# Small first groups and a denser opening weave in a sparse graph-attention layer

## The chip, the core and the metric

The kernel runs on one core of a Trainium2 chip. The metric is the device time of one execution in microseconds (us); lower is better. The engines are PE (TensorE, matrix products), DVE (VectorE), ACT (ScalarE), POOL (GpSimd) and SP (SyncE, which here only issues transfers). Each takes its own instructions strictly in the order in which the program lists them, and waits for the others through semaphores.

## The reference, cut to what matters

One layer of graph attention over 4096 nodes with 512 features, and then a norm. A target row attends to the source rows that `adj` connects it to: about 16 of 4096, itself included.

```python
hs = layer_norm(h_source); ht = layer_norm(h_target)        # h_source is x
q, k, v = ht @ Wq, hs @ Wk, hs @ Wv                          # 8 heads of 64
logits = einsum('thd,shd->hts', q / 8, k), -1e30 where adj == 0
ctx = einsum('hts,shd->thd', softmax(logits), v)
ht = layer_norm(ht + ctx @ Wo)
ht = ht + gelu(ht @ W1) @ W2                                 # 512 -> 2048 -> 512
out = _layernorm(x + ht)
```

Everything is float32.

## The kernel before

**Stages.** In the first 280 us PE computes the rows of keys and values of all 4096 source nodes and ACT writes them to a table in memory, `kvd` (4 KB for each node: key, then value). Beside this the kernel reads the dense `adj` and makes a list of neighbours of each target row; the rows of the first half of the targets (part A) are then sorted by their number of neighbours and cut into 16 tiles of 128 rows. A tile has a cap, the largest number of neighbours in it. The tiles are taken in the order of caps 11, 13, 14, 15, 15, 16, 17, 17, 18, 19, 19, 20, 22, 23, 24, 39 and then the 16 tiles of part B. Tiles are numbered from 0 in this order.

**Attention of a tile** (`attention`, with `front`, `issue`, `values` and `finish`). For each neighbour slot POOL issues one gather of 128 rows of `kvd` (L987, 512 KB) into a ring of slots, 17 of them for part A. Three slots make a segment. For a segment DVE multiplies keys with the query `tq` (L1258) and sums over each head (L1263); ACT takes the exponent (L1267, or L1276 for a tile's first segment); DVE multiplies two slots' values with it (L1219), and ACT the third slot's, head by head (`by_scalar`, L1239 and L1242). PE adds the values up by transposing them into one PSUM tile, `cps` (L1230, four for each slot), and only after that may the slot be gathered into again. The query comes from `front`: a gather (L987, `tq`), two PE steps (transposes L1030, product with `wq` L1040) and an add on DVE (L1045).

**The end of a tile** is `finish`: sums and reciprocal on DVE (L1115, L1118, L1121, L1122), a copy on ACT (L1125), four PE transposes (L1131), a copy on ACT (L1133), the scaling on DVE (L1136), the product with `wo` on PE (L1142, L1146), a copy on ACT (L1151) and the statistics of the norm on DVE (L697, L698). When the last tile of a group is there, the norm follows: L680 on DVE, a power on POOL (L687), L692 on DVE, L1164 on ACT, transposes on PE (L1173) and a copy into `h2T` on ACT (L1177).

**Feed-forward of a group** (`feed`). `_order` makes the groups: the first tile alone, then pairs. A group's `h2T` goes through W1 (L1367, `pf`), gelu on ACT (L1370) and W2 (L1376, into `po`), and `end` adds `x`, norms and writes the rows out. A pair has eight blocks with 256 columns, a group of one has four with 128 columns.

**Order.** No engine chooses. `_weave` runs four generators (attention, feed-forward, the lists of the rest of part B, the last weight loads) in the order of a written clock: each `yield` tells how much the piece before it costs, and the generator with the least sum is next. A pair's attention costs 60 (`UNIT`), and so does its feed-forward; a feed-forward whose `h2T` isn't made yet sleeps. `yield`s without a number inside `finish` and `front` put their next step behind further attention work. After that a scheduler fixes each engine's list; `tc.issue_after` (here `behind`) puts an instruction behind another on its engine. `other_lists` starts at clock 94 (`WAIT`), and each of its steps costs 2.2 times its own figure. `weights` loads the third quarter of W1 and W2 at clock 26 and the fourth at 36, each as two transfers of 1 MB from ACT's queue.

Of the kernel before, what the change touches and what calls it, by code (L numbers as in the profile page):

```python
# [12 lines left out]
ALU = mybir.AluOpType  # L13
# [371 lines left out]
def _order():  # L385


    n, m = len(CAPS_A), len(CAPS_B)
    a = [(k * P, c) for k, c in enumerate(CAPS_A)]
    b = [((n + k) * P, c) for k, c in enumerate(CAPS_B)]  # L390
    groups = [[a.pop()]]
    while len(a) > 1:
        groups.append([a.pop(), a.pop()])
    groups.append(a + [b.pop()])
    while len(b) > 1:
        groups.append([b.pop(0), b.pop()])
    return groups + [b]
# [46 lines left out]
def adj_resnorm_kernel(  # L444
# [88 lines left out]
    with tc.tile_pool(name="keep", bufs=1) as keep:  # L533
# [17 lines left out]
        with ExitStack() as late:  # L551
# [429 lines left out]


            recs, tqs, h2Ts, done, ready, latest, newest = {}, {}, {}, set(), [], [], []
            issues, logits = [], []

            def gather(dst, table, idx):
                issues[:] = [nc.gpsimd.indirect_dma_start(  # L987
# [121 lines left out]
            def finish(i, p, cps, group, hs, mv):  # L1109


                rec, tq, cap = recs[i], tqs.pop(i), TILES[i][1]
                slow = 0 if i < QUICK else 1

                nc.vector.scalar_tensor_tensor(p[:, :cap, :], rec[:, E0:E0 + cap].unsqueeze(2)  # L1115
                                               .to_broadcast([P, cap, H]), 0.0, p[:, :cap, :],
                                               op0=ALU.is_gt, op1=ALU.mult)
                nc.vector.tensor_reduce(sums[:, i, :], p[:, :cap, :].rearrange("p j h -> p h j"),  # L1118
                                        AX.X, ALU.add)
                ri = sp.tile([P, H], F32, name="ri")  # L1120
                nc.vector.tensor_scalar_max(ri, sums[:, i, :], SUM_LO)  # L1121
                nc.vector.reciprocal(ri, ri)  # L1122
                rx = sp.tile([P, KC, P], F32, name="rb", bufs=1)
                rxf = rx.rearrange("p c t -> p (c t)")
                nc.scalar.copy(rxf.rearrange("p (h d) -> p h d", h=H),  # L1125
                               ri.unsqueeze(2).to_broadcast([P, H, HD]))
                for _ in range(1 + 1 * slow):
                    yield
                prx = ps.tile([P, KC, P], F32, name="t", bufs=2)
                for c in range(KC):  # L1130
                    nc.tensor.transpose(prx[:, c, :], rxf[:, c * P:(c + 1) * P], ident)  # L1131
                ct = sp.tile([P, KC, P], F32, name="rb", bufs=1)
                nc.scalar.copy(ct, prx)  # L1133
                for _ in range(1 + 1 * slow):
                    yield
                nc.vector.tensor_mul(ct, cps, ct)  # L1136
                for _ in range(1 + 3 * slow):
                    yield
                pa = ps.tile([P, D], F32, name="t", bufs=2)

                for c in range(KC):
                    nc.tensor.matmul(pa[:, c * P:(c + 1) * P], tq[:, D + c * P:D + (c + 1) * P],  # L1142
                                     ident, is_transpose=True, start=c == 0, stop=False,
                                     skip_group_check=True)
                for c in range(KC):
                    nc.tensor.matmul(pa, ct[:, c, :], wo[:, c, :], start=False,  # L1146
                                     stop=c == KC - 1, skip_group_check=True)
                turned.add(i)
                yield
                h = sp.tile([P, D], F32, name="h")  # L1150
                nc.scalar.copy(h, pa)  # L1151
                yield
                stats(sp, h, mv[:, len(hs), :], "n2")
                hs.append(h)
                if len(hs) < len(group):
                    return
                nh = len(hs)
                ve = shifted(sp, mv[:, :nh, :], nh, "n2")
                yield
                rs = power(sp, mv[:, :nh, :], nh, "n2", ve)  # L1160
                yield
                nm = negmean(sp, mv[:, :nh, :], rs, nh, "n2")
                for j, h in enumerate(hs):
                    nc.scalar.activation(h, h, AF.Identity, bias=nm[:, j:j + 1], scale=rs[:, j:j + 1])  # L1164
                for _ in range(1 + 1 * slow):
                    yield
                w = len(hs) * P
                h2T = sp.tile([P, KC, 2 * P], F32, name="h2T")
                for k2 in range(KC // 2):
                    pt = ps.tile([P, 2, 2 * P], F32, name="t", bufs=2)  # L1170
                    for k in range(2):
                        for j, h in enumerate(hs):
                            nc.tensor.transpose(pt[:, k, j * P:(j + 1) * P],  # L1173
                                                h[:, (k2 * 2 + k) * P:(k2 * 2 + k + 1) * P], ident)
                    for k in range(2):
                        kc = k2 * 2 + k
                        nc.scalar.activation(h2T[:, kc, :w], pt[:, k, :w], AF.Identity,  # L1177
                                             bias=b2c[:, kc:kc + 1], scale=s2c[:, kc:kc + 1])
                h2Ts[GROUPS.index(group)] = h2T
# [22 lines left out]
            def attention():  # L1202
# [44 lines left out]
                for group in GROUPS:  # L1247
                    hs = []
                    mv = sp.tile([P, 2, 2], F32, name="mv2")
                    cost = 0.5 * UNIT * len(group) / 2 / sum(TILES[i][1] for i in group)  # L1250
                    for i in group:
                        cps = ps.tile([P, KC, P], F32, name="cps", bufs=2)
                        while k < len(SG) and SG[k][0] == i:
                            _, j0, n = SG[k]
                            while i not in tqs:
                                step(fronts, i)
                            kv, tq = kvs.pop(k), tqs[i]
                            nc.vector.tensor_tensor(kv[:, :n, :D], kv[:, :n, :D],  # L1258
                                                    tq[:, :D].unsqueeze(1).to_broadcast([P, n, D]),
                                                    ALU.mult)  # L1260
                            lg = sp.tile([P, S, H], F32, name="lg")
                            latest[:] = [lg[:, 0, 0:1]]
                            logits[:] = [nc.vector.tensor_reduce(  # L1263
                                lg[:, :n, :], kv[:, :n, :D].rearrange("p j (h d) -> p j h d", h=H),
                                AX.X, ALU.add).ins]
                            if j0 > 0:
                                nc.scalar.activation(p[:, j0:j0 + n, :], lg[:, :n, :], AF.Exp)  # L1267
                            advance()
                            yield cost * n
                            if pend:  # L1270
                                values(*pend.pop())
                                request(k)
                            advance()
                            if j0 == 0:
                                p = sp.tile([P, MAXE, H], F32, name="p", bufs=1)
                                nc.scalar.activation(p[:, :n, :], lg[:, :n, :], AF.Exp)  # L1276
                            if n == S:
# [142 lines left out]
                for g in gens:  # L1420
                    yield from g

            WAIT = 94.0
            AHEAD = 4
            ADDS = 11
            HEAVY = 30
            DENSE = 21
            QUICK = 7
            UNIT = 60.0

            ed = all_edges()
            steps = 2 * NQ + 1
# [57 lines left out]
            def weights():  # L1490


                for q, pool in enumerate(pools):
                    yield 26.0 if q == 0 else 10.0
                    with tc.issue_after(newest[-1]):
                        load_quarter(pool, q + 2, nc.scalar)

            def other_lists():
                for _ in range(2):
                    adjs.append(quarter(*divmod(len(adjs), NQ)))  # L1500
                yield 6.0
                for cost in ed:
                    yield 2.2 * cost
                keep_rest()
                yield from sort(1)

# [37 lines left out]
```

## Time and profile before

| | us |
|---|---|
| median of 3 runs (1791.04 to 1794.76) | 1792.74 |
| the profiled execution | 1786.53 |
| its span in the trace | 1784.8 |
| PE, DVE, ACT, POOL busy in the span | 1663.4, 1422.9, 1236.9, 1005.6 |
| POOL's gathers of `kvd`, 603 of them | 785.6 |

The profiled execution ran 1.7 us beside its span, and 6.2 us (0.35%) under the median of the runs shown. Busy times are unions of recorded spans on one engine. Matmul records overlap, since the next one starts before the last has left the array; a stretch in which PE is busy all the time is one in which it never waited, but the record's length isn't what a matmul costs. That cost is the distance between two starts in a row of equal matmuls. Each float32 product is recorded as two matmuls; a transpose is one.

### The profile page before, as it was taken

Reading aid. Unit: us, or ns where it says so; the run is one execution under the profiler, and the core shown is the slowest. Engines: PE = TensorE matmul, PEld = TensorE weight load, DVE = VectorE, ACT = ScalarE, POOL = GpSimd, SP = SyncE. Lnnn points to the kernel's source line nnn. Section 1 sums busy time; section 2 is a strip of 40 time slices with the busy share of each in tenths; the row PEclk is TensorE's granted clock in tenths of the full one; section 3 lists DMA queues with packets and bytes.
Section 4 is the critical chain, followed back from the end, with each engine's and each line's share of the span. In section 5 each row is a group of like instructions: output and inputs, shape, how many; then the busy total and the mean of one; then the engine's idle time right before and its main releaser. Section 6 shows DMA issues by size and latency. Waiting matters only on the chain. (4 is left out here: it accounts for less than half of the span.)

```text
span 1784.8 us, 22466 instructions
## 1 busy us (share of the span) xinstructions
PE 1663.4 (93%) x6850; PEld 1074.3 (60%) x6850; DVE 1422.9 (80%) x2447; ACT 1236.9 (69%) x3131; POOL 1005.6 (56%) x822
## 2 busy tenths in 40 slices
PE   7989994889999999898888999999999999999997
PEld 3434443656666766665555766666666666656665
DVE  6888787879688989897878888989888888987500
ACT  5776663667777878676667877787878777876511
POOL 1000156765556666677777688866686766665101
PEclk9999997899999999999999999999999999999999
DMA  9999988978778798767777798987777867665000
GB/s 350 362 391 367 360 269 304 336 242 282 268 256 299 272 316 277 248 205 252 243 273 272 244 316 286 304 278 237 246 257 247 298 218 255 233 230 189 20 5 26
DMA packets 141610, 461.00 MB, mean 258 GB/s; under 512 B 18036, under 2 KB 23048, under 8 KB 141480
## 3 DMA queue, kind: packets, MB, share of 16 engines
q0 software_dynamic: 96272, 342.33, 56.6%
q1 hardware_dynamic: 37392, 94.06, 14.8%
q10 hardware_dynamic: 7816, 23.08, 3.3%
q8 instruction: 57, 0.93, 0.2%
q14 instruction: 73, 0.60, 0.1%
HBM read 430.61 MB, written 28.79 MB: 257 GB/s over the span
## 5 line engine op out<-in xcount | busy, mean ns | idle before, releaser
L987 POOL DMA_INDIRECT kv<-kvd,rec x603 | 785.6, 1303 | 342.2 <-issue 117.4
L1367 PE MATMUL pf<-h2T,w 128*128 128x256 f32 (+1 forms) x2176 | 473.7, 371 | 3.4 <-ACT h2T L1177 3.4
L1376 PE MATMUL po<-w,gt 128*128 128x512 f32 x1024 | 465.4, 596 | 2.7 <-ACT gt L1370 2.7
L1367 PEld LDWEIGHTS pf<-h2T,w 128*128 128x128 f32 x2176 | 391.1, 193 | 72.5 <-issue 22.2
L1258 DVE TENSOR_TENSOR kv<-kv,tq 128x1536 f32<-128x1536 f32 (+2 forms) x211 | 351.9, 1677 | 66.7 <-DMA kv<-kvd,rec 54.0
L1242 ACT ACTIVATE kv<-kv,pa 128x64 f32<-128x64 f32 x1520 | 390.7, 336 | 4.4
L1263 DVE TENSOR_REDUCE lg<-kv 128x24 f32<-128x1536 f32 (+2 forms) x211 | 350.4, 1667 | 0.3
L1376 PEld LDWEIGHTS po<-w,gt 128*128 128x128 f32 x1024 | 188.2, 191 | 196.8 <-issue 192.8
L1230 PE MATMUL cps<-ident,kv 128*128 128x128 f32 x1828 | 245.6, 280 | 51.9 <-DVE kv L1219 34.1
L1230 PEld LDWEIGHTS cps<-ident,kv 128*128 128x128 f32 x1828 | 216.7, 144 | 127.6 <-DVE kv L1219 40.6
L1219 DVE TENSOR_TENSOR kv<-kv,p 128x1024 f32<-128x1024 f32 (+1 forms) x211 | 251.2, 1192 | 25.2 <-ACT p L1267 23.7
L687 POOL TENSOR_TENSOR n_rs<-n_ve,mhalf 128x2 f32<-128x2 f32 (+2 forms) x51 | 53.5, 1049 | 338.7 <-DVE n_ve L680 155.1
L735 ACT ACTIVATE kv<-kv 128x1024 uint8<-128x1024 int32 x128 | 134.5, 1053 | 60.1 <-DMA kv<-in_adj_dram 24.3
L1370 ACT ACT_TABLE_LOAD x109 | 139.8, 1283 | 1.8
L1370 ACT ACTIVATE gt<-pf 128x512 f32<-128x512 f32 x128 | 76.4, 597 | 88.2 <-PE pf L1367 84.9
L1146 PE MATMUL t<-wo,rb 128*128 128x512 f32 x256 | 120.0, 610 | 7.9 <-DVE rb L1136 7.9
L949 PE MATMUL pq<-wk,h2T 128*128 128x512 f32 x256 | 118.8, 607 | 4.2 <-DMA wk<-in_L_gnn_Wk_dram 2.9
L949 PE MATMUL pq<-wv,h2T 128*128 128x512 f32 x256 | 117.3, 601 | 4.2 <-DVE rbc L662 2.9
L1040 PE MATMUL t<-wq,tq 128*128 128x512 f32 x256 | 115.4, 593 | 2.4 <-ACT tq L1033 2.4
L744 DVE MAX8 cand<-kv 128x8 uint16<-128x171 uint16 (+1 forms) x384 | 108.0, 324 | 1.2
L1267 ACT ACTIVATE p<-lg 128x24 f32<-128x24 f32 (+2 forms) x179 | 39.0, 218 | 100.3 <-DVE lg L1263 99.4
L1267 ACT ACT_TABLE_LOAD x71 | 91.1, 1283 | 1.2
(164 smaller groups left out, 1534.6 us busy)
## 6 DMA issues: line engine op xcount, KB each, us to landing
kv<-in_adj_dram SPq DMA_DIRECT2D x128, 512.0 KB, 6.8
kvd<-tq ACTq DMA_DIRECT2D x23, 512.0 KB, 7.0
kv<-kvd,rec POOLq DMA_INDIRECT x603, 5.9
kv<-in_L_gnn_h_target_dram SPq DMA_DIRECT2D x32, 256.0 KB, 7.2
kv<-in_x_dram SPq DMA_DIRECT2D x15, 512.0 KB, 8.3
kvd<-kv ACTq DMA_DIRECT2D x9, 512.0 KB, 7.0
w<-in_L_gnn_W_dram SPq DMA_DIRECT2D x4, 1024.0 KB, 7.2
w<-in_L_gnn_W_dram ACTq DMA_DIRECT2D x4, 1024.0 KB, 15.4
```

Source lines behind the costliest of these rows:

```text
L735: nc.scalar.activation(sg, a, AF.Sign, accum_out=dpart[:, i, h:h + 1])
L949: nc.tensor.matmul(pkv, hT[:, kc, j * P:(j + 1) * P], w[:, kc, :], start=kc == 0, stop=kc == KC - 1)
L987: issues[:] = [nc.gpsimd.indirect_dma_start(out=dst, out_offset=None, in_=table[:, :], in_offset=bass.IndirectOffsetOnAxis(ap=idx, axis=0) ...
L1219: nc.vector.tensor_tensor(v4, v4, p[:, j0:j0 + m, :].unsqueeze(3) .to_broadcast([P, m, H, HD]), ALU.mult)
L1230: nc.tensor.matmul(cps[:, c, :], kv[:, j, D + c * P:D + (c + 1) * P], ident, is_transpose=True, start=j0 + j == 0 and c == 0, stop=j0 + n ...
L1242: newest[:] = [nc.scalar.mul(v, v, pa[:, hd:hd + 1]).ins]
L1258: nc.vector.tensor_tensor(kv[:, :n, :D], kv[:, :n, :D], tq[:, :D].unsqueeze(1).to_broadcast([P, n, D]), ALU.mult)
L1263: logits[:] = [nc.vector.tensor_reduce(lg[:, :n, :], kv[:, :n, :D].rearrange("p j (h d) -> p j h d", h=H), AX.X, ALU.add).ins]
L1267: nc.scalar.activation(p[:, j0:j0 + n, :], lg[:, :n, :], AF.Exp)
L1367: nc.tensor.matmul(pf[:, k, :], w1[(f0 + k) // KC][:, kc, (f0 + k) % KC * P:((f0 + k) % KC + 1) * P], h2T[:, kc, :w], start=kc == 0, stop= ...
L1370: nc.scalar.activation(gt, pf, AF.Gelu_apprx_tanh)
L1376: nc.tensor.matmul(po[j], gt[:, k, j * P:(j + 1) * P], w2[(f0 + k) // KC][:, (f0 + k) % KC, :], start=False, stop=f0 + k == FC - 1, skip_g ...
```

## The change

Five edits.

1. `_order` makes three groups of one tile (0, 1 and 2) and then pairs. Groups are now 0 / 1 / 2 / 3,4 / 5,6 and so on: the pair 1,2 is split, and from 3,4 on every group holds the same tiles as before. There is one group more, 18 for 17.
2. In `finish`, tile 0 has no `yield` between its first steps, and tiles 0 to 2 have two fewer later.
3. Tile 0's reciprocal and scaling are remembered in `closing`; the next product of keys is put behind the reciprocal, the next sum over heads behind both, and then the list is emptied.
4. For groups that start with tiles 1 to 8, the clock's cost of attention is multiplied by 0.7 (tiles 1 to 4) or 0.85 (tiles 5 to 8).
5. `WAIT` goes from 94 to 70, the factor of the lists from 2.2 to 1.9, and the fourth quarter of the weights follows the third after 6 and not 10.

```diff
-    groups = [[a.pop()]]
+    groups = [[a.pop()] for _ in range(3)]
     while len(a) > 1:
         groups.append([a.pop(), a.pop()])
...
+                first = i == 0
...
-                nc.vector.reciprocal(ri, ri)
+                recip = nc.vector.reciprocal(ri, ri)
...
-                for _ in range(1 + 1 * slow):
+                for _ in range(0 if first else 1 + slow):
                     yield
...
-                nc.vector.tensor_mul(ct, cps, ct)
-                for _ in range(1 + 3 * slow):
+                scaled = nc.vector.tensor_mul(ct, cps, ct)
+                if first:
+                    closing[:] = [recip.ins, scaled.ins]
+                for _ in range(0 if first else 1 + 3 * slow):
                     yield
...
                 turned.add(i)
-                yield
+                if i > 2:
+                    yield
...
                 ve = shifted(sp, mv[:, :nh, :], nh, "n2")
-                yield
+                if i > 2:
+                    yield
...
                     cost = 0.5 * UNIT * len(group) / 2 / sum(TILES[i][1] for i in group)
+                    if 0 < group[0] < 9:
+                        cost *= PACE[group[0] > 4]
...
-                            nc.vector.tensor_tensor(kv[:, :n, :D], kv[:, :n, :D],
-                                                    tq[:, :D].unsqueeze(1).to_broadcast([P, n, D]),
-                                                    ALU.mult)
+                            with behind(closing[:1]):
+                                nc.vector.tensor_tensor(kv[:, :n, :D], kv[:, :n, :D],
+                                                        tq[:, :D].unsqueeze(1)
+                                                        .to_broadcast([P, n, D]), ALU.mult)
...
-                            logits[:] = [nc.vector.tensor_reduce(
+                            with behind(closing):
+                                logits[:] = [nc.vector.tensor_reduce(
...
+                            closing.clear()
...
-            WAIT = 94.0
+            WAIT = 70.0
+            PACE = (0.7, 0.85)
...
-                    yield 26.0 if q == 0 else 10.0
+                    yield 26.0 if q == 0 else 6.0
...
-                    yield 2.2 * cost
+                    yield 1.9 * cost
```

More of the change, by code (lines that the diff above doesn't have):

```diff
@@ L983, in adj_resnorm_kernel @@
             recs, tqs, h2Ts, done, ready, latest, newest = {}, {}, {}, set(), [], [], []
-            issues, logits = [], []
+            issues, logits, closing = [], [], []
             def gather(dst, table, idx):
@@ L1133, in finish @@
                 nc.scalar.copy(ct, prx)
-                for _ in range(1 + 1 * slow):
+                for _ in range(0 if first else 1 + slow):
                     yield
-                nc.vector.tensor_mul(ct, cps, ct)
-                for _ in range(1 + 3 * slow):
+                scaled = nc.vector.tensor_mul(ct, cps, ct)
+                if first:
+                    closing[:] = [recip.ins, scaled.ins]
+                for _ in range(0 if first else 1 + 3 * slow):
                     yield
@@ L1164, in finish @@
                     nc.scalar.activation(h, h, AF.Identity, bias=nm[:, j:j + 1], scale=rs[:, j:j + 1])
-                for _ in range(1 + 1 * slow):
+                for _ in range(0 if first else 1 + slow):
                     yield
@@ L1257, in attention @@
                             kv, tq = kvs.pop(k), tqs[i]
-                            nc.vector.tensor_tensor(kv[:, :n, :D], kv[:, :n, :D],
-                                                    tq[:, :D].unsqueeze(1).to_broadcast([P, n, D]),
-                                                    ALU.mult)
+                            with behind(closing[:1]):
+                                nc.vector.tensor_tensor(kv[:, :n, :D], kv[:, :n, :D],
+                                                        tq[:, :D].unsqueeze(1)
+                                                        .to_broadcast([P, n, D]), ALU.mult)
                             lg = sp.tile([P, S, H], F32, name="lg")
                             latest[:] = [lg[:, 0, 0:1]]
-                            logits[:] = [nc.vector.tensor_reduce(
-                                lg[:, :n, :], kv[:, :n, :D].rearrange("p j (h d) -> p j h d", h=H),
-                                AX.X, ALU.add).ins]
+                            with behind(closing):
+                                logits[:] = [nc.vector.tensor_reduce(
+                                    lg[:, :n, :],
+                                    kv[:, :n, :D].rearrange("p j (h d) -> p j h d", h=H),
+                                    AX.X, ALU.add).ins]
+                            closing.clear()
                             if j0 > 0:
```

## The prediction

> **What bounds the kernel now.** I read the page's slices first, then a table by stretches, then PE's timeline.
>
> ```profile
> PE   7989994889999999898888999999999999999997
> PEclk9999997899999999999999999999999999999999
> ```
>
> PE is nearly full to the end. The table has, for each stretch, its length and then busy us of PE, weight loads, DVE, ACT and POOL, the granted clock and the DMA share.
>
> ```profile
> 280.00:340.00 60.00, 30.71 (x145) 22.30 (x145) 45.88 (x46) 22.93 (x86) 42.95 (x36) 0.74 0.98 369
> 340.00:380.00 40.00, 40.00 (x225) 28.32 (x224) 28.45 (x29) 24.96 (x69) 23.51 (x20) 1.00 0.62 198
> 380.00:405.00 25.00, 18.32 (x94) 12.93 (x93) 23.43 (x42) 19.52 (x62) 21.14 (x15) 0.85 0.93 336
> 405.00:500.00 95.00, 92.17 (x403) 63.08 (x401) 76.48 (x142) 68.68 (x171) 50.45 (x45) 0.97 0.75 260
> 500.00:590.00 90.00, 90.00 (x409) 62.67 (x408) 77.04 (x134) 69.42 (x181) 57.14 (x47) 1.00 0.82 288
> 740.00:1080.00 340.00, 302.37 (x1347) 208.94 (x1346) 286.84 (x306) 238.24 (x668) 259.37 (x201) 0.96 0.77 260
> 1080.00:1640.00 560.00, 551.17 (x2316) 364.62 (x2315) 488.59 (x560) 427.91 (x1112) 393.60 (x309) 1.00 0.77 256
> 1640.00:1773.00 133.00, 132.68 (x555) 87.91 (x553) 39.33 (x94) 48.02 (x112) 10.23 (x12) 1.00 0.06 20
> ```
>
> PE never waits in 340 to 380, 500 to 590 and after 1640; it waits in 280 to 340, in 380 to 405 and in 740 to 1080, and its clock is then cut too. So the span is PE's work plus PE's lost time, and the change is worth the lost time that it removes. What the work costs is read from PE's timeline, by distances between starts:
>
> ```profile
> 358.88 3.60 PE L1376 MATMUL po<-w,gt 128*128 128x512 f32 x8
> 362.31 1.47 PE L1230 MATMUL cps<-ident,kv 128*128 128x128 f32 x12
> 363.62 3.74 PE L1367 MATMUL pf<-h2T,w 128*128 128x128 f32 x32
> 367.20 3.60 PE L1040 MATMUL t<-wq,tq 128*128 128x512 f32 x8
> ...
> 419.63 3.62 PE L1367 MATMUL pf<-h2T,w 128*128 128x256 f32 x16
> 423.08 1.47 PE L1230 MATMUL cps<-ident,kv 128*128 128x128 f32 x12
> ```
>
> (362.31-358.88)/8 is 0.429 us at 512 columns; likewise 0.109 for a transpose, 0.112 for a product of 128 columns and 0.216 for 256. Multiplying by the counts gives the work ahead of each group's first L1367; start minus work is the time lost by then:
>
> | group | starts | work ahead | lost |
> |---|---|---|---|
> | 0 | 338.0 | 268.6 | 69.4 |
> | 1,2 | 405.3 | 325.8 | 79.5 |
> | 3,4 | 498.7 | 413.1 | 85.6 |
> | 5,6 | 586.8 | 500.9 | 85.9 |
> | 7,8 | 679.9 | 591.1 | 88.8 |
> | 9,10 | 780.7 | 680.4 | 100.3 |
> | last | 1744.4 | 1585.7 | 158.7 |
>
> **What the Trainium skill says.** "Perfetto Trace Analysis", section "Identifying the Most-Contended Engine", calls matmul busy time no good measure; agreed: eight L1376 records of 0.592 us each sit in 3.43 us, hence the distances. "TensorE: Matmul & The Clock Gate", Part 1, "What's actually happening", says that PE's clock halves after an idle window of some 3.4 us; the table shows 0.74 and 0.85 in the two stretches with waits and 1.00 in the full ones. "DMA: Bandwidth & Descriptors", "Queues, rings and completion order", says that an engine takes turns between queues; here ACT's four weight transfers landed after 15.4 us (median) beside gathers, SP's four of the same size after 7.2 us.
>
> **The change, part by part.** I had the order in which each engine of the changed kernel gets its instructions; durations are the profile's. Lines are the kernel's before.
>
> *First tile's end.* DVE's timeline before:
>
> ```profile
> 307.52 1.79 DVE L1258 TENSOR_TENSOR kv<-kv,tq 128x1536 f32<-128x1536 f32 x1 [1.36 <-DMA kv<-kvd,rec]
> 309.24 0.19 DVE L1122 RECIPROCAL ri<-ri 128x8 f32<-128x8 f32 x1
> ...
> 321.41 1.76 DVE L1258 TENSOR_TENSOR kv<-kv,tq 128x1536 f32<-128x1536 f32 x1 [2.31 <-DMA kv<-kvd,rec]
> 323.37 0.69 DVE L1258 TENSOR_TENSOR kv<-kv,tq 128x512 f32<-128x512 f32 x1 [0.20 <-DMA kv<-kvd,rec]
> 323.98 0.68 DVE L1136 TENSOR_TENSOR rb<-cps,rb 128x512 f32<-128x512 f32 x1
> ```
>
> The reciprocal now stands ahead of the product that waits for a gather: 3 us earlier. But the scaling L1136 still stands behind **all four** remaining products of tile 1, the last of which had its data at 323.4; only the sums were moved behind it. With one L1219 (1.22) in between it comes at 325.1, 1.1 us later than before. Then come what was done earlier before: two sums (3.4), two small steps and L1219, a sum, L697, L1219, a sum, L1219. This puts tile 1's fourth segment at 336.5 (it was 328). PE has 44 of tile 1's transposes ahead of L1173; POOL has four gathers ahead of the power, whose slots come free late (power at about 337, was 333.6). So L692 is at 337.7, L1164 ends at 338.7, the copies to `h2T` at 340.9: the first block starts at **341, 3 us later**.
>
> *Tile 2's query.* L1030 and L1040 were ahead of the first block and are now behind its start and behind its 64 matmuls (7.2 us): work ahead is 264.3. L1040 ends at 352 and not 335.8, so tile 2's attention starts 16 us later. Behind it on DVE wait tile 2's products. Lost by the first block: 341-264.3 = 76.7, against 69.4.
>
> *Groups of one.* Before, PE at 380 to 405 has nothing, as 1,2 wait for tile 2. Now PE goes on from 352: W2, two blocks, tile 1's end, tile 2's first three segments, tile 3's query; by distances that is until 386, and each of these has its input in time (tile 2's DVE work from 352.7: values of its segments at 362.8 and 365.7). The norm of tile 1 is ready at about 384, `h2T` at 388, so group 1 starts at 388.5 with 310.1 ahead: lost 78.4. Tile 3's query is ready at 381.9 (371.5 before), tile 4's at 416 (399.7). DVE needs 35.4 us for tile 3 (five segments of 4.7, nine from the lists, the ends 3); PE has 43 us for a tile (28 feed-forward, 6.9 for the two 512-column products, 6.5 for 15 slots, 2 other transposes). So PE stays the slower and group 3,4 starts at 413.3+78.4 = 491.7, **7 us earlier** than 498.7.
>
> *The split pair* costs 2 x 128 x 0.112 against 128 x 0.216: +1.0 us on PE. Gelus are as many; ACT's table loads go from 220 to 224 in the whole program, 1.28 us each, beside a full PE: nothing while ACT isn't late.
>
> POOL gets two powers more (L687, 0.66 us each for one column), and its gathers queue behind each: now behind the 45th, 53rd, 58th and 73rd gather, where it was the 62nd and 69th. The one after 58 waits for tile 2's norm, some 410 by the above; tile 4's second segment, which is behind it, isn't wanted before 420: nothing, +6 at most if that norm is late.
>
> *Denser weave.* From 5,6 on PE's order is nearly the same, except that feed-forward starts up to 10 us of work further behind its `h2T` (5,6: 9.9, was 5.6; 13,14: 19.0, was 10.7). That leaves blocks to fill a wait such as the one at 677 (2.74 us for `h2T`, then half clock, 4.5 lost in 660 to 690): I take -4. The bounds are 0 and -10, all waits for the norm between 590 and 1000.
>
> *Lists and weights.* The clock shifts cancel: the lists' DVE steps stand behind the 17th to 62nd segment (18th to 62nd before), POOL's sixteen scatters behind 204 to 255 gathers (208 to 255), SP's reads of `adj` likewise. Nothing for the sum, -5 to +5 for the 740 to 1080 stretch, where each wait is a gather's and a small shift moves it. The fourth quarter's two transfers leave 9 us earlier on the same ACT queue, with the third's two just ahead; what is moved by 325 is the same. Nothing, -2 to +2 for tile 1's last gather. The end (1640 on) is the same work: nothing.
>
> Sum: -7.2 (85.6 to 78.4) + 1.0 - 4 = **-10**. The profiled execution would be 1776 after 1786.5, the median 1782.5 after 1792.7.
>
> **Rivals.** *Gain eaten:* the first tile's end isn't ahead, so the edit does not do what it says; a few us more at 300 to 341 and again before group 1 and -10 is -3 to +3. For it: the late first block; against: the wait at 380 to 405, which splitting the pair plainly removes. About 1792. *Slower:* the late query makes attention the bound. Tile 2 starts 16 us late and by tile 4 still 16; if a tile takes ACT or DVE over 43 us there, PE waits for 3,4 instead of leading. Each us over 43 for tiles 3 and 4 counts twice; at 52, group 3,4 is 18 us later than I say, +11 on the old start and +8 in the sum: 1801. It decides from 48 us on. For it: every tile's end adds waits between engines that busy times don't show; against: DVE is at 76 and ACT at 69 of 95 us in 405 to 500, and the ends of tiles 3 and 4 (L1115) were only 28 us apart, at 408 and 436. *More:* also the 740 to 1080 waits shrink, as attention leads: -20, 1773.
>
> **How the numbers follow.** A measurement of this kernel tells 0.2%, 3.6 us, from no change. Chances: forecast 0.55, more 0.1, eaten 0.14, slower 0.21. Faster 0.66 (with a few of the eaten), same 0.13, slower 0.21. Range 1768 to 1798: the sum's bounds on both sides and most of the slow case; at most 0.2 is left out.
>
> **What would show it.** Right: first L1367 near 341, second group near 388, PE full from 341 to 590, 3,4 near 492, the same 159 lost later less the gain. Wrong: a wait on PE between 390 and 490 for L1219 or `h2T` (slower), the second group after 400 (eaten), or a new wait past 740.

## The result, and the profile after

| | before | after |
|---|---|---|
| median, 22 runs each on one chip | 1793.82 us | 1789.63 us |
| ratio, 95% interval | | 0.9963 [0.9948, 0.9979] |
| profiled execution / its span | 1786.53 / 1784.8 us | 1787.19 / 1785.4 us |

The forecast was 1782.5 us, in a range of 1768 to 1798. In this measurement the change is a gain of 0.2 to 0.5%, where the forecast was 0.56%. The changed kernel was measured twice more beside the kernel before (second and third occasion below), and gave 0.9993 [0.9978, 1.0009] and 0.9992 [0.9977, 1.0008]; neither is told from no change. Over all three the ratios are between no change and a gain of 0.4%. A ratio here is an estimate over all runs of both kernels, with its interval; it is not the quotient of the two medians, which can lie up to 0.14% beside it. The two profiled executions do not show a gain at all; that of before was the fastest of its 22 runs, 7.3 us under their median. So what follows is argued from where each trace loses its time, not from the two spans.

First the slices of the page after, the same two rows as before. The seventh and eighth slice (268 to 312 and 312 to 357 us) of PE are now 6 and 6 where they were 4 and 8, and its clock in the eighth is a 7 for an 8; the first tile's end and tile 1 lie here. Beyond them a digit goes up here and down there.

```profile
PE   7999986699899999998889998999999999999997
PEclk9999997799999999999999999999999999999999
```

The table by stretches of the changed kernel (length, busy us of PE, weight loads, DVE, ACT, POOL, then clock, DMA share, GB/s) says more:

```profile
280.00:340.00 60.00, 29.18 (x120) 19.64 (x120) 41.08 (x40) 20.62 (x82) 40.86 (x35) 0.69 0.95 346
340.00:380.00 40.00, 39.42 (x228) 28.67 (x229) 25.76 (x31) 26.11 (x68) 20.52 (x18) 1.00 0.55 185
380.00:405.00 25.00, 25.00 (x154) 18.72 (x153) 21.55 (x26) 19.05 (x45) 15.99 (x16) 1.00 0.79 259
405.00:500.00 95.00, 89.42 (x496) 62.95 (x495) 84.48 (x163) 75.57 (x204) 61.71 (x51) 0.96 0.85 294
500.00:590.00 90.00, 87.46 (x398) 60.59 (x398) 79.61 (x127) 69.39 (x178) 53.39 (x45) 0.98 0.82 284
740.00:1080.00 340.00, 307.93 (x1374) 212.29 (x1375) 288.83 (x307) 238.88 (x674) 261.67 (x206) 0.96 0.80 264
1080.00:1640.00 560.00, 547.61 (x2288) 362.97 (x2287) 484.48 (x559) 429.54 (x1104) 400.42 (x302) 0.99 0.76 251
```

The wait at 380 to 405 is gone: PE is busy 25.00 of 25 us, where it was 18.32. But 405 to 500 went from 92.17 to 89.42, 500 to 590 from 90.00 to 87.46, and 1080 to 1640 from 551.17 to 547.61. Of the other stretches shown only 740 to 1080 is better, by 5.6. A wait taken away in one stretch came back in the next ones.

**Lost time, kernel by kernel.** This is the prediction's sum (start of a group's first feed-forward product, minus PE's work ahead of it by the distances between starts), counted anew in one way for all profiled executions, so the rows of before differ by up to 0.7 us from the prediction's table. For after, the work ahead is 264.6, 358.1 (group 2), 413.6 (3,4), 682.2 (9,10), 950.7 (15,16) and 1587.4 (the last). Executions of one kernel differ by 1 us (after) to 7 us (hold_products) in the column of the last group.

| kernel | start of group 0 | lost: group 0 | ahead of 3,4 | 3,4 | 9,10 | 15,16 | last | start of 3,4 |
|---|---|---|---|---|---|---|---|---|
| before | 338.0 | 69.1 | 79.2 | 85.3 | 99.6 | 140.1 | 158.1 | 498.7 |
| before, again | 338.6 | 69.7 | 78.7 | 84.4 | 97.5 | 133.2 | 154.6 | 497.8 |
| after | 341.6 | 77.0 | 77.5 | 85.4 | 97.5 | 141.4 | 158.1 | 498.9 |
| after, again | 340.7 | 76.1 | 78.1 | 85.0 | 97.2 | 140.9 | 156.9 | 498.6 |
| after, third | 340.7 | 76.1 | 77.1 | 84.0 | 96.5 | 143.0 | 158.2 | 497.6 |
| split_only | 339.8 | 70.9 | 73.4 | 86.0 | 101.2 | 139.9 | 161.1 | 498.9 |
| clock_only | 344.6 | 75.6 | 79.7 | 94.0 | 103.5 | 145.8 | 158.7 | 515.5 |
| no_split | 341.5 | 76.9 | 86.7 | 92.1 | 103.9 | 146.1 | 159.1 | 507.9 |
| old_clock | 335.6 | 70.9 | 78.1 | 92.9 | 108.6 | 145.6 | 166.3 | 507.6 |
| no_hold | 337.2 | 72.0 | 73.0 | 79.7 | 93.6 | 140.0 | 156.7 | 493.2 |
| hold_products | 334.0 | 69.4 | 70.5 | 77.2 | 87.0 | 130.9 | 147.6 | 490.8 |
| hold_products, again | 335.5 | 70.9 | 73.6 | 81.2 | 94.9 | 140.4 | 154.9 | 494.7 |
| hold_rec8 | 336.8 | 72.2 | 75.0 | 83.9 | 94.4 | 139.4 | 153.9 | 497.5 |
| rec_sp | 342.1 | 77.5 | 78.1 | 84.9 | 99.4 | 144.4 | 159.5 | 498.5 |

Read the first rows from left to right. After has lost 6 to 8 us more than before by its first block. By the group ahead of 3,4 it has made that up and 1 to 2 us besides: this is the wait at 380 to 405. Then it loses 7 to 8 us on the way to 3,4, as before lost 6, and **group 3,4 starts where it started before**.

**What PE waits for ahead of 3,4.** The line of PE's timeline that answers to it, first of the kernel before, then of after (start, length, instruction, and the wait before it with its releaser):

```profile
469.93 5.09 PE L1146 MATMUL t<-wo,rb 128*128 128x512 f32 x8 [2.64 <-DVE rb L1136]
```
```profile
481.00 5.50 PE L1149 MATMUL t<-wo,rb 128*128 128x512 f32 x8 [5.47 <-DVE rb L1137]
```

Both kernels wait here for the scaling at the end of tile 4, before its product with `wo`. After waits 5.47 us and then runs the eight products in 5.50 instead of 3.60 us, because its clock is down (0.67 granted from 481.0 to 486.5, 1.00 from there on). 5.5 and 1.9 make the 7.4 of the 7.9 us that the table shows between group 2 and 3,4.

The way back from there, from DVE's, ACT's and again DVE's timeline of the changed kernel:

```profile
461.00 1.78 DVE L1266 TENSOR_TENSOR kv<-kv,tq 128x1536 f32<-128x1536 f32 x1 [4.59 <-DMA kv<-kvd,rec]
```
```profile
464.48 0.22 ACT L1287 ACTIVATE p<-lg 128x24 f32<-128x24 f32 x1 [9.25 <-DVE lg L1272]
...
470.20 1.28 ACT L1244 ACT_TABLE_LOAD   x1
...
479.65 0.58 ACT L1134 COPY rb<-t 128x512 f32<-128x512 f32 x1
```
```profile
480.26 0.69 DVE L1137 TENSOR_TENSOR rb<-cps,rb 128x512 f32<-128x512 f32 x1
```

The scaling needs the copy L1134, which ACT reaches at 479.65. Tile 4's reciprocal was ready at 451.4, so the end of tile 4 was never short of numbers, only of its turn. PE had made the transposes that L1134 copies by 470.35, so the copy stood 9.3 us in ACT's queue; in the kernel before it stood there 5.1 us (462.08 to 467.13). ACT did nothing for 9.25 us up to 464.48, for want of tile 5's first sum. DVE had that segment's product at 454.65, but the sum stands behind the next segment's product on DVE, and that one waited until 461.00 for its gather. From 466.14 on ACT has no gap until the copy; three table loads of 1.28 us, one of them shown, lie in between, two of them for gelus. The Trainium skill's page "ScalarE: Activation LUTs", section "What ACT_TABLE_LOAD costs", gives 1283 ns for the load, which this trace has too, and 1380 ns of draining beside it; here the next instruction starts 1.29 us after the load does (470.20 to 471.49), so no drain is seen.

And what stands ahead of that gather, the second segment's: POOL's timeline of the changed kernel, the last column again the wait and its releaser.

```profile
444.45 1.47 POOL L687 TENSOR_TENSOR n_rs<-n_ve,mhalf 128x1 f32<-128x1 f32 x1 [0.44 <-DVE n_ve L1339]
449.37 0.61 POOL L1001 DMA_DIRECT2D rec<-rec  x1 [3.45 <-DVE p L1116]
450.28 1.02 POOL L1351 DMA_INDIRECT out_dram<-xt,tags  x1 [0.31 <-issue]
451.61 0.99 POOL L987 DMA_INDIRECT kv<-kvd,rec  x1 [0.30 <-PE t L1040]
```

The power belongs to the last norm of group 1, a group that did not exist before, and behind it stand the load of a tile's records and that group's write; the gathers from 451.61 on stand behind all three. From 424 up to this power every wait of POOL was 0.44 us or less. Whether a place of the end of tile 4 ahead of tile 5's exponents on ACT would take PE's wait away was not tried.

### The profile page after: what moved, and what is told of

The parts are those of the page before. It is cut to its first block, busy times and chain, and to the rows that moved or that the text cites. A ratio compares the mean times of both kernels' runs of the same rounds, so it can differ in the third digit from the quotient of the medians.

```text
span 1785.4 us, 22727 instructions
## 1 busy us (share of the span) xinstructions
PE 1661.0 (93%) x6978; PEld 1076.3 (60%) x6978; DVE 1425.7 (80%) x2452; ACT 1241.9 (70%) x3139; POOL 1020.4 (57%) x824
## 5 line engine op out<-in xcount | busy, mean ns | idle before, releaser
L687 POOL TENSOR_TENSOR n_rs<-n_ve,mhalf 128x2 f32<-128x2 f32 (+2 forms) x53 | 57.4, 1083 | 316.2 <-DVE n_ve L680 143.4
L1381 ACT ACT_TABLE_LOAD x111 | 142.4, 1283 | 1.9
L1040 PE MATMUL t<-wq,tq 128*128 128x512 f32 x256 | 116.9, 600 | 5.3 <-ACT tq L1033 5.3
L949 PEld LDWEIGHTS pq<-wv,h2T 128*128 128x128 f32 x256 | 49.4, 195 | 74.2 <-issue 59.8
```

What stands on the lines that cost most here:

```text
L949: nc.tensor.matmul(pkv, hT[:, kc, j * P:(j + 1) * P], w[:, kc, :], start=kc == 0, stop=kc == KC - 1)
L1381: nc.scalar.activation(gt, pf, AF.Gelu_apprx_tanh)
```

## The experiments

Three occasions after the measurement above; the kernels of one occasion ran on one chip beside the same runs of before (1787.47, 1786.53 and 1788.68 us). Ratios are to these. The changed kernel itself did not run on the first of them, so its parts can be set beside the whole only by ratios of different occasions. Edit 2 was in no run taken out or put in alone.

### First occasion: the parts of the change

**split_only**: before with edit 1 alone.

```diff
-    groups = [[a.pop()]]
+    groups = [[a.pop()] for _ in range(3)]
```

> The kernel before with edit 1 alone (three groups of one tile; clock, ends and order of DVE as before). Theory A (the gain is the wait before group 1,2 that the split removes): the first block starts near 338 as before, group 1 no later than 382, PE has lost at most 78 us when group 3,4 starts (85.6 before), and the time is at least as good as with the whole change: 5 to 10 us under before, ratio 0.994 to 0.997. Theory B (the gain is the denser clock, which lets feed-forward blocks trail and fill later waits): no gain, ratio 0.999 to 1.001.

Measured: 1787.52 us, 1.0003 [0.9991, 1.0015]. The split takes the wait at 380 to 405 away (73.4 us lost by group 2, against 79.2), and the next 70 us give it all back: 86.0 lost by 3,4, which starts at 498.9. PE's timeline of this kernel shows the longest of the waits that come in its place, before the transposes of the values that DVE has yet to make:

```profile
494.68 2.82 PE L1230 MATMUL cps<-ident,kv 128*128 128x128 f32 x12 [3.35 <-DVE kv L1219]
```

So the theory that the wait before group 1,2 is by itself the gain falls: in this trace attention, not PE, sets the start of 3,4.

**no_split**: after with edit 1 undone.

```diff
-    groups = [[a.pop()] for _ in range(3)]
+    groups = [[a.pop()]]
```

> The changed kernel with edit 1 undone (1,2 a pair again; the rest of the change stays). Theory A: no gain or a loss, since group 1,2 waits for a tile 2 that starts some 14 us later than before: its first block at 405 to 420, ratio 1.000 to 1.008. Theory B: the gain of the whole change stays, ratio 0.996.

Measured: 1784.24 us, 0.9976 [0.9962, 0.9989]. Without the split there is still a gain, though 92.1 us are lost by 3,4. In the trace it would have to come later: from 3,4 to the last group it loses 67.0 us, where before loses 72.8 and 70.2 in its two executions. That fits blocks that trail further behind their input and so wait less later, but it does not prove it: at the last group this execution has lost as much as before (159.1 and 158.1), and at 1787.47 us it is one of the slower runs of its kernel.

**no_hold**: after without edit 3.

```diff
-                    closing[:] = [recip.ins, scaled.ins]
+                    pass
```

> The changed kernel without edit 3 (nothing is held behind the first tile's reciprocal or scaling). Theory A: the hold brings nothing, as the scaling stands behind all of tile 1's products with it and behind four with or without it: the scaling within 2 us of 327.5, the first block within 3 us of 341.6, ratio 0.995 to 0.998. Rival D (the hold is what wins): ratio 0.999 or more.

Measured: 1781.94 us, 0.9970 [0.9959, 0.9981]. The hold isn't needed for a gain. The scaling comes at 322.9 and the first block at 337.2, both earlier than theory A expected (near 327.5 and 341.6), so with the denser clock the hold as written costs some 4 us at the opening: it keeps tile 1's sums back but not the products that wait for gathers. At the last group the lost time is after's again (156.7), so the lead is not kept in this trace.

**hold_products**: the hold put where it was said to be. The scaling stands ahead of tile 1's products from its third segment on, and no sum is held.

```diff
-                            with behind(closing):
-                                logits[:] = [nc.vector.tensor_reduce(
...
-                            closing.clear()
+                            logits[:] = [nc.vector.tensor_reduce(
...
+                            del closing[:-1]
+                            if i > 1:
+                                closing.clear()
```

> The changed kernel, but on DVE tile 1's products from its third segment on stand behind the first tile's scaling, and no sum is held. Theory A: the scaling runs at 313 to 316 and not at 327.5, the first block starts at 330 to 335 (341.6 with the change) as PE still has 44 of tile 1's transposes ahead of it, tile 2's query follows 7 us earlier, and 4 to 8 us more are won: ratio 0.992 to 0.994. Rival C (the opening is slack, as the stage after it is bound by gathers): the first block moves and the time does not, ratio 0.996.

Measured: 1778.20 us, 0.9959 [0.9942, 0.9975]. DVE's timeline of this kernel, and then that of after:

```profile
306.67 0.20 DVE L1123 RECIPROCAL ri<-ri 128x8 f32<-128x8 f32 x1
...
312.91 0.68 DVE L1137 TENSOR_TENSOR rb<-cps,rb 128x512 f32<-128x512 f32 x1
314.58 1.76 DVE L1266 TENSOR_TENSOR kv<-kv,tq 128x1536 f32<-128x1536 f32 x1 [0.98 <-DMA kv<-kvd,rec]
321.28 1.76 DVE L1266 TENSOR_TENSOR kv<-kv,tq 128x1536 f32<-128x1536 f32 x1 [4.95 <-DMA kv<-kvd,rec]
```
```profile
309.72 0.20 DVE L1123 RECIPROCAL ri<-ri 128x8 f32<-128x8 f32 x1
310.88 1.76 DVE L1266 TENSOR_TENSOR kv<-kv,tq 128x1536 f32<-128x1536 f32 x1 [0.96 <-DMA kv<-kvd,rec]
317.99 1.76 DVE L1266 TENSOR_TENSOR kv<-kv,tq 128x1536 f32<-128x1536 f32 x1 [5.35 <-DMA kv<-kvd,rec]
324.06 1.76 DVE L1266 TENSOR_TENSOR kv<-kv,tq 128x1536 f32<-128x1536 f32 x1 [4.31 <-DMA kv<-kvd,rec]
...
327.48 0.69 DVE L1137 TENSOR_TENSOR rb<-cps,rb 128x512 f32<-128x512 f32 x1
```

From the reciprocal to the scaling it is 6.2 us here and 17.8 us in after, where three products wait 10.6 us for gathers in between. With the scaling ahead of them DVE waits for the same gathers, but the first tile's end is already out. The first block comes at 334.0 and not at 341.6, and 3,4 at 490.8. Theory A had the times of the scaling and the block right; the ratio is the 0.996 of rival C, though the trace keeps the lead to the end (147.6 us lost).

### Second occasion: repeats, the clock, and a first try at POOL's stall

**before_again**, one execution of the kernel before, unchanged:

> The kernel before, profiled a second time. If its first profiled execution (6 to 7 us under its median) was an unusually good one, this one loses more on PE than 158.1 us by the last group's first block, and says where; if the lost time is the same again, the difference of the medians has to lie outside what PE's lost time tells.

One run, 1783.11 us, span 1781.4. It gives the second row of the table and so the size of what two executions differ by: 1 us up to 3,4, 6.9 us at 15,16 and 3.5 at the last group. It loses less than the first one and not more, so the first was not an unusually good one by its lost time.

**after_again**, unchanged:

> The changed kernel again, on the chip that the next two run on. All theories: ratio 0.995 to 0.998. Theory B, which the split alone (no gain) and the rest alone (0.9976) favour: lost time at group 3,4 stays near 85, and the gain is made after it, in waits that trailing feed-forward blocks fill.

Measured: 1786.67 us, 0.9993 [0.9978, 1.0009]. The starts agree with the first profile to 1 us, up to 3,4; the gain is not repeated.

**old_clock**: after with edits 4 and 5 undone.

```diff
-            WAIT = 70.0
+            WAIT = 94.0
...
-            PACE = (0.7, 0.85)
+            PACE = (1.0, 1.0)
...
-                    yield 26.0 if q == 0 else 6.0
+                    yield 26.0 if q == 0 else 10.0
...
-                    yield 1.9 * cost
+                    yield 2.2 * cost
```

> The changed kernel with edits 4 and 5 undone (old clock for attention, lists and weights). Theory B (the denser clock is needed for the gain): no gain, ratio 0.998 to 1.001, the feed-forward of 3,4 starting at 495 or later. Rival A (the groups of one and the earlier end suffice): ratio 0.996 or less.

Measured: 1794.14 us, 1.0042 [1.0025, 1.0059]. Beside after on the same chip, the denser clock is worth 7.5 us, once edits 1 to 3 are in. It is also slower than the kernel before, which neither theory expected. The place is not where the prediction put it (blocks from 5,6 on) but ahead of 3,4: 92.9 us lost there against 85.0, a difference of 7.9. PE's longest wait there is 4.25 us up to 491.39. The profile names no releaser for it, but it ends when ACT has scaled the query that PE transposes next (L1026, done at 491.34), and ACT had before that waited 3.00 us for a read of `adj`. So the lists may have a part in it; edits 4 and 5 were not separated.

At the opening the denser clock does the opposite. Here, with edit 3 in, the scaling stands ahead of tile 1's last two products and not behind all four, as DVE's timeline shows, and the first block starts at 335.6, earlier than in before:

```profile
319.45 0.68 DVE L1137 TENSOR_TENSOR rb<-cps,rb 128x512 f32<-128x512 f32 x1
...
323.84 1.76 DVE L1266 TENSOR_TENSOR kv<-kv,tq 128x1536 f32<-128x1536 f32 x1 [0.18 <-DMA kv<-kvd,rec]
```

**hold_rec8**: hold_products with eight buffers for a tile's records.

```diff
-                rec = sp.tile([P, E0 + MAXE], I32, name="rec", bufs=6)
+                rec = sp.tile([P, E0 + MAXE], I32, name="rec", bufs=8)
```

> hold_products with eight buffers for rec in place of six, nothing else. Theory E: the wait on PE before tile 4's product with wo (5.5 us with the change, 4.5 in hold_products) comes from POOL: the load of rec waits 3.45 us for a buffer, and the gathers behind it are late. Without that wait PE loses 5 to 7 us less by group 3,4 (70 to 73, hold_products 77.2), and the ratio is 0.989 to 0.993. Rival: the gathers wait for slots or bandwidth anyway; then the wait stays and the ratio is that of hold_products, 0.996.

Measured: 1784.71 us, 0.9989 [0.9976, 1.0002]. The theory that the record load waits for a free buffer fell: the load still waits 2.55 us for L1116, PE waits 6.57 us at 479.57, and 3,4 starts at 497.5. More buffers brought nothing; the ratio even lies above that of hold_products (0.9959 and 0.9960, intervals apart), which neither side expected, and why stays open.

### Third occasion: POOL again, the clock alone, and both versions side by side

**rec_sp**: after with the record loads of tiles 6 to 15 on SP's queue.

```diff
-                (nc.sync if part and i < NT - 4 else nc.gpsimd).dma_start(rec[:, :RW], recs_d[part][r0:r0 + P, :])
+                (nc.sync if (i < NT - 4 if part else i > 5) else nc.gpsimd).dma_start(rec[:, :RW], recs_d[part][r0:r0 + P, :])
```

> The changed kernel with one edit: the loads of the tiles' records (L1001) for tiles 6 to 15 are issued from SP's queue and not from POOL's. In the changed kernel one of these loads holds POOL still from 445.9 to 449.4 (3.45 us), and behind it wait the write of the output and all gathers of tile 5. Theory E' (POOL's stall there is what makes the scaling of tile 4 late, 480.3, and PE's wait of 5.5 us before tile 4's product with Wo): tile 5's gathers start about 4 us earlier, PE's wait before that product falls from 5.5 to 2 us or less, group 3,4 starts at 491 to 495 and not at 498.9, and the time is 3 to 6 us under the changed kernel's of the same chip. Theory F (POOL is bound by issuing in that stretch, one gather in 1.25 us with no gap, and DVE waits for the gathers of tile 4 that stand ahead of the stall): the wait stays at 4 to 6 us, group 3,4 starts within 2 us of 498.9, and the time is within 2 us of the changed kernel's.

Measured: 1795.47 us, 1.0041 [1.0027, 1.0055]. As to the wait, 3,4 is at 498.5 and PE waits 4.08 us at 480.20, so E' fell. But F isn't shown by that, since the stall did not go. POOL's timeline of this kernel:

```profile
446.48 0.59 POOL L687 TENSOR_TENSOR n_rs<-n_ve,mhalf 128x1 f32<-128x1 f32 x1
450.14 1.05 POOL L1351 DMA_INDIRECT out_dram<-xt,tags  x1 [3.08 <-ACT xt L1347]
451.50 0.97 POOL L987 DMA_INDIRECT kv<-kvd,rec  x1 [0.30 <-issue]
```

(The expectation calls all gathers of tile 5 late; its first segment's had been issued before, the second's is meant.) With the load gone, the write of group 1 waits for ACT's last step of that group, which needs the power just ahead of it, and the gathers start at 451.50 instead of 451.61. What holds the queue is the pair of power and write, with a trip over DVE and ACT between them; the record load only stood in that gap.

The 8.3 us by which this kernel is slower than after lie elsewhere, after the last write. Its lost time at the last group is 159.5, as in after (158.2), but its span ends 49.9 us after that group's start and not 39.8. SP's queue waits there for PE's at the end of the program; the waits of SP in rec_sp (us in all, times, longest):

```profile
SPq L1551 <- PEq L1551: 8.8, 2, 8.3
```

In the third run of after the longest of these two waits is 0.5 us. No work stands in it. What PE's queue waits for isn't shown, and it stays open.

**clock_only**: before with edits 4 and 5 alone.

```diff
+                    if 0 < group[0] < 9:
+                        cost *= PACE[group[0] > 4]
...
-            WAIT = 94.0
+            WAIT = 70.0
+            PACE = (0.7, 0.85)
...
-                    yield 26.0 if q == 0 else 10.0
+                    yield 26.0 if q == 0 else 6.0
...
-                    yield 2.2 * cost
+                    yield 1.9 * cost
```

> The kernel before with edits 4 and 5 alone (PACE 0.7 and 0.85 for the groups from 1,2 to 7,8; WAIT 70; 1.9; 6); the groups stay 0 / 1,2 / 3,4, and the first tile's end is as before. Theory B (the denser clock is the part that pays, with or without the split): 4 to 8 us under the kernel before, ratio 0.996 to 0.998, with less lost from group 11,12 on. Rival G (the clock pays only together with the split, since both early pieces compete for PE at 340 to 500): within 2 us of the kernel before or slower. Rival H (the split and the earlier end are worth something of their own beside the clock): this kernel is 2 to 4 us slower than the changed kernel on the same chip.

Measured: 1790.67 us, 1.0013 [0.9997, 1.0029]; after on the same chip 1787.15. The clock alone does not pay. With more attention put ahead of the blocks and no group of one to fill PE, PE comes to tile 4's product with `wo` with nothing to do:

```profile
468.53 5.20 PE L1146 MATMUL t<-wo,rb 128*128 128x512 f32 x8 [12.29 <-DVE rb L1136]
```

At the opening the first block comes at 344.6, 6 us later than in before. Theory B fell for the clock on its own. The times fit G and H (2.0 us slower than before, 3.5 slower than after, with overlapping intervals), but G's reason, that the clock needs the split, does not fit no_split: there the clock gained without the split, beside edits 2 and 3 (0.9976, on another chip).

**hold_products_again** and **after_third**, unchanged:

> Second look at the kernel with the changed hold: the first tile's scaling stands ahead of the products of tile 1 from its third segment on, and no sum is held. The first time it was at 0.9959 of the kernel before, with the first block at 334.0 and not at 341. If the gain of the earlier first block lasts to the end, it is again 3 to 9 us under the changed kernel of the same chip and its lost time at the last group is 148 to 152; if that was the luck of one chip, within 2 us of the changed kernel.

> The changed kernel once more, unchanged, as the partner of the other three on this chip. It gave 0.9963 and 0.9993 of the kernel before on two occasions. Expected 0.996 to 0.999, with the first block at 341, group 3,4 at 498.5 to 499 and 156 to 159 us lost at the last group.

Measured: 1783.85 us, 0.9960 [0.9946, 0.9974], and 1787.15 us, 0.9992 [0.9977, 1.0008]. The version with the changed hold repeats its ratio (0.9959 before), and its interval ends below the point where after's begins. It beats the kernel before twice and the changed kernel once, by 3.3 us between medians. Its lost time at the last group, 154.9, is 3.3 under after's and not in the 148 to 152 that were expected.

## Why the prediction was right or wrong, point by point

**The sign was right; the size was near only once, and the two gains of its sum were not found.** Forecast -10; the three measurements gave 0.9963, 0.9993 and 0.9992, by these ratios -6.6, -1.3 and -1.4 us of some 1790. The -7.2 ahead of 3,4 did not come, and the -4 is seen in no trace of after. That the first measurement lies near the forecast is luck as far as these runs tell.

*First tile's end: right in the number, in part by luck.* First block forecast at 341 with 76.7 us lost; it came at 341.6, 340.7 and 340.7 with 77.0, 76.1 and 76.1. The scaling came at 327.5, 2.4 us later than the 325.1 of the working, as the last products waited for their gathers longer than in before, and the reciprocal came at 309.72, not 3 us ahead of before's 309.24. The later steps were 1.7 to 1.9 us late as well (L1169 ends at 340.5, the copies to `h2T` at 342.6), but the block started with the first of the four copies and not after the last, and the two errors cancel. That edit 3 does not put the scaling ahead of the products, as the prediction said, hold_products shows from the other side: do it, and the block is at 334.0 and 335.5. But what makes the block later than in before is not edit 3 alone: with edits 1 to 3 and the old clock (old_clock) it starts at 335.6, with the denser clock alone (clock_only) at 344.6.

*Tile 2's query and group 1: right.* L1040 ends at 352.8 (352). Group 1 starts at 387.6, 386.7 and 386.8 (388.5), and PE is full from 380 to 405.

*"So PE stays the slower and group 3,4 starts at 413.3+78.4 = 491.7": wrong*, by 7 us (498.9, 498.6, 497.6), and this was the -7.2 of the sum. Of that -7.2, only 1.1 came from the wait before 1,2 as the table counts it (79.5 to 78.4 lost). The other 6.1 was the step from 79.5 to 85.6 in the prediction's own table, which lies between 405 and 500. The prediction let it vanish without naming what made it, and left that stretch out where it listed PE's waits, though its table has PE busy for 92.17 of 95 us there. Part of the step did belong to the removed wait, since PE's clock was still down behind it (0.50 from 405 to 407). PE's timeline before:

```profile
405.27 8.47 PE L1367 MATMUL pf<-h2T,w 128*128 128x256 f32 x32
```

The next instruction starts at 413.57, so these 32 products cost 8.3 us and not 32 x 0.216 = 6.9, which is 1.4 of the 6.1. The larger part, 4.1, was the wait for tile 4's scaling (2.64 us at 469.93) and the lower clock behind it (1.5). The argument put in its place, DVE 35.4 us and PE 43 us for a tile, compares sums of busy time; the tile's end is a chain through DVE, ACT, PE, ACT and DVE, each step in its turn in a queue. This second wait did not go but became longer.

The measure of this chain is the distance between the starts of group 0 and of 3,4. In the eight executions that have groups of one and the denser clock (the three of after, no_hold, the three with the changed hold, rec_sp) it is, in this order, 157.3, 157.9, 156.9, 156.0, 156.8, 159.2, 160.7 and 156.4 us, while PE has 149.0 us of work there (148.4 in no_hold). In these, a first block 4.4 to 7.6 us ahead of after's 341.6 goes with a start of 3,4 that is 1.4 to 8.1 us ahead of 498.9. So an earlier end of the first tile carries through to 3,4, though not always in full: that is what hold_products gains, and what after lacks, having its first block 3 us later than before.

*POOL's two powers, "nothing, +6 at most if that norm is late": not settled.* The term was sized by the powers of the norm that feeds a group. The stall that the trace has, 5 us with the write, comes from the power and the write that close group 1. Two tries to take it away did not take it away, so whether it makes tile 4's scaling late, or would be followed by another wait, stays open.

*The split pair, +1.0: right.* PE's work in the span went from 1614.8 to 1615.9 us.

*Denser weave, -4 from the blocks of 5,6 and later: wrong in place.* From 3,4 to the last group after loses 72.7, 71.9 and 74.2 us, before 72.8 and 70.2. Its stretch 740 to 1080 has less waiting, but two waits stand at 1017 and 1085 (3.78 us for ACT's `tq`, 4.44 for a gelu), and by group 15,16 the lead is gone. Ahead of 3,4, where the prediction gave it nothing, the same clock (with edit 5) saves 7.9 us of lost time beside old_clock, which is 7.5 us slower.

*Lists and weights, nothing:* not shown, since only edits 4 and 5 together were undone. The read of `adj` that ACT waits for in old_clock's trace is a sign against it.

*The rivals.* "Gain eaten" had the right outcome in two measurements of three (1786.67 and 1787.15 beside 1786.53 and 1788.68), by a wait in another place than the one it named. "Slower" had the right mechanism, a late tile 4 that PE waits for, at a price of 7 us and not of 18. What made the first measurement better than the other two by 5 us isn't explained by any trace here.

## What to carry to other kernels

A wait of the engine that sets the time is worth what the next wait behind it leaves: ask which later start is held by a chain that does not begin at this wait, and if its input comes no earlier, neither does the end. When a table of lost time is used as a forecast, each step of it that is to vanish needs a wait with a name and a reason why it goes. An instruction that closes a chain should stand ahead of those that wait for transfers, and the order on the engine, not the intent of the edit, tells whether it does.

## What the runs showed of the hardware that was not expected

PE's clock can go down after a shorter wait than expected. The eight products of 512 columns are a gauge: they take 3.70 us after a short wait, and over 5 us when the clock is down for part of them. Over the fourteen profiled executions, from 20 us on, 104 such rows follow a wait of PE of less than 2.09 us; 100 of them took 3.70, and the other four follow another wait of PE closely. After 2.09 to 3.17 us both occur: 14 rows of 41 took 3.70, the others 5.1 to 6.7. After more than 3.17 us none of 33 took less than 5.08. Beside the line of before at 469.93 above (5.09 us long after a wait of 2.64), one on the other side, from PE's timeline of no_split:

```profile
1090.07 3.70 PE L1040 MATMUL t<-wq,tq 128*128 128x512 f32 x8 [2.50 <-ACT tq L1033]
```

The Trainium skill's page "TensorE: Matmul & The Clock Gate", Part 1, speaks of an idle window of some 3.4 us. Here a wait of 2.1 to 3.2 us was enough in 27 cases of 41, and then and after longer waits the lower clock adds 1.4 to 3.1 us (5.08 to 6.77, less 3.70) to the wait. The wait of 2.50 us cost 2.5, that of 2.64 in the kernel before cost 4.0.
